# The order of the 24 attention-times-value products inside a unit: h's products by a table of four orders for each place, l's products drawn at random

## The chip, the cores and the metric

The kernel runs on one core of one Trainium2 chip. The metric is the device time of one execution in microseconds, the median of several. The core's engines run their own instruction streams side by side: TensorE (PE, with its weight loads shown apart as PEld), VectorE (DVE), ScalarE (ACT), GpSimd (POOL) and SyncE (SP); the last two issue most of the DMA transfers here.

## What is computed

For each of B = 4 images, with N = 64 x 64 = 4096 positions and C = 256 channels:

```python
q = einsum('bwhc,cd->bwhd', x, Wq) + bq      # d = 128
k = einsum('bwhc,cd->bwhd', x, Wk) + bk
v = einsum('bwhc,cd->bwhd', x, Wv) + bv      # d = 256
pq, pk, pv = q.reshape(B, -1, N), k.reshape(B, -1, N), v.reshape(B, -1, N)
energy = einsum('bcn,bcm->bnm', pq, pk)
attention = softmax(energy, axis=-1)
out = einsum('bcm,bnm->bcn', pv, attention).reshape(B, W, H, C)
return gamma * out + x
```

All of it is in float32. The kernel uses TensorE's faster float32 form (`F32R`) and gets its accuracy back by splitting numbers into parts: the attention weights of a unit are held as three tiles h, l and d, and the values as three arrays `vh`, `vl` and `vd`.

## The kernel before

**Tiling.** An image's 4096 output columns are cut into 16 groups of 256 (`NG`, `NB`; two halves j of 128, `NJ` = 2). For every group the 4096 positions m that are summed over are gone through in 8 units (`NU`) of four blocks of 128 positions each. So an image has 128 units (`STEPS`) and the program 512. A unit's number in its group, t = u mod 8, is called its *place*.

**What a unit does.** TensorE makes 12 products for the energies of the unit three ahead (`energy`, line 330, 256 columns each), and 24 products in `attend` (line 383): eight with weights from h, eight from l, eight from d. ScalarE takes the exponentials of the energies (line 334) and makes h (line 349); VectorE joins the two exponentials (line 344) and makes l (line 355) and d (line 358). GpSimd's queue loads the next k tile (line 314).

**The 24 products.** Each is one load of 128x128 weights and one matmul. The weights are `left[:, i, j*P:(j+1)*P]`: block i of 0 to 3, half j of 0 or 1. What streams through them is one row of the value array, `right[:, m, ...]` with `m = 2*t + i//2 + 16*(i%2)`; both halves j of a block i stream the same row. For h and l the row is 258 columns wide (256 values and two ones, which sum up the softmax's denominator) and goes to `acc[j]`, a PSUM tile for each half; for d it is 256 wide and goes to `bb`. `vh` and `vl` hold rows of `VC` = 260 float32, that is 1040 bytes, so that a row's start, in bytes, is 16 m beyond a multiple of 1024; `vd` holds rows of 256 float32, 1024 bytes, so that all its rows start alike. Blocks i = 0 and 1 of a unit (m = 2t and 2t + 16) start equally far, modulo 256 bytes, and i = 2 and 3 (m = 2t + 1 and 2t + 17) start 16 bytes further; they are called L and H below.

**The order before.** For each of h, l, d: first half j = 0 with i = 0, 1, 2, 3, then j = 1 with i = 0, 1, 2, 3. Written as digits x = 4 j + i this is 01234567, as starts it is LLHHLLHH. One exception is written in the code (`back`): in l's products of places 1 and 3 the second half goes i = 3, 2, 1, 0.

**What sets the order around it.** The whole kernel runs under a manual schedule: each engine's queue holds its instructions in the order in which the program writes them. In the loop over units (lines 509 to 551) it is: energies of u + 3, first half; join and upper of u + 2; energies, second half; load of k; a piece of an earlier group's `finish`; `halves` of u + 1; `attend(u)`; another piece of `finish`. At a group's last unit (t = 7) ScalarE copies `acc[0]` and `acc[1]` out (line 394). The pieces of `finish` then run on the other engines: VectorE reads `bb` (line 404) in the next unit, ScalarE scales (line 407), and TensorE transposes the result (line 415) after `attend` of place 1. `finish_last` (lines 427 to 464) does the same for the very last group.

Of the kernel before, what the change touches and what calls it, by code (L numbers as in the profile page):

```python
# [2 lines left out]

# [17 lines left out]
def kernel(  # L21
# [36 lines left out]
    nc = tc.nc  # L58
    B, W, H, C = x.shape
    P = 128  # L60
# [4 lines left out]
    NI = NM // 2  # L65
# [108 lines left out]
    NJ = NB // P  # L174
    NG = N // NB
    NU = NM // 4
# [22 lines left out]
    with ExitStack() as fast:  # L199
# [18 lines left out]
        vh = qkv.tile([P, NM, VC], F32R, tag="vh", name="vh")  # L218
        vl = qkv.tile([P, NM, VC], F32R, tag="vl", name="vl")
        vd = qkv.tile([P, NM, C], F32R, tag="vd", name="vd")  # L220
# [131 lines left out]
        def halves(b, u):  # L352
# [7 lines left out]
            )  # L360
            units[b, u] = h, l, d

        def attend(b, u):

            g, t = divmod(u, NU)
            if t == 0:
                now["acc"] = [
                    ps_o.tile([P, C + 2], F32, tag=f"a{j}", name=f"a{j}_{b}_{g}")
                    for j in range(NJ)
                ]  # L370
                now["bb"] = ps_o.tile([P, NJ, C], F32, tag="bb", name=f"bb_{b}_{g}")
            h, l, d = units[b, u]
            acc, bb = now["acc"], now["bb"]
            for left, right in ((h, vh), (l, vl), (d, vd)):
                for j in range(NJ):
                    out_ = bb[:, j, :] if left is d else acc[j]


                    back = left is l and j == NJ - 1 and t in (1, 3)
                    for i in reversed(range(4)) if back else range(4):  # L380
                        m = 2 * t + i // 2 + NI * (i % 2)

                        nc.tensor.matmul(  # L383
                            out_,
                            left[:, i, j * P : (j + 1) * P],
                            right[:, m, : out_.shape[1]],
                            start=(t == i == 0 and (left is h or left is d and j == 0)),
                            stop=(t == NU - 1 and i == 3 and left is not h),
                            skip_group_check=True,
                        )  # L390
            if t == NU - 1 and (b, g) != (B - 1, NG - 1):
                o = now["o"] = work.tile([P, NJ, C + 2], F32, tag="o", name=f"o_{b}_{g}")
                for j in range(NJ):
                    nc.scalar.activation(o[:, j, :], acc[j], AF.Identity, scale=1.0 + E)
# [89 lines left out]
        for b in range(B):  # L484
# [24 lines left out]
            for u in range(STEPS):  # L509
                g, t = divmod(u, NU)  # L510
# [33 lines left out]
                for forms in beside:  # L544
                    next(forms)
                attend(b, u)
                if (b, u) == (B - 1, STEPS - 1):
                    finish_last(b, g, loads.pop((b, "x", g)))
# [10 lines left out]
    NG = N // NB  # L559
    NJ = NB // P  # L560
    NP = NM // 2
    xg, og = columns(x, NB), columns(out, NB)
    with tc.If(nc.values_load(again[0:1, 0:1]) > 0), ExitStack() as general:
# [8 lines left out]
        for b in range(B):  # L572
# [16 lines left out]
            for g in range(NG):  # L589
                ps = []  # L590
                mx = work.tile([P, 2, NB], F32, tag="mx", name=f"gmx_{b}_{g}")
                for t in range(NP):
                    sp = ps_s.tile([P, 2, NB], F32, tag="s", name=f"gs_{b}_{g}_{t}")
                    for h in range(2):
# [4 lines left out]
                            start=True,  # L599
                            stop=True,  # L600
# [31 lines left out]
                for t, p in enumerate(ps):  # L632
# [8 lines left out]
                    for h in range(2):  # L641
                        for s in range(2):
# [4 lines left out]
                                start=(t == h == 0),  # L647
                                stop=(2 * t + h == NM - 1),
# [43 lines left out]
```

## Time and profile before

| what | value |
|---|---|
| median of 8 runs | 2449.4 us (2447.75 to 2450.61) |
| the profiled execution's own time | 2449.84 us |
| span of its trace, first to last instruction | 2448.1 us |
| mean granted TensorE clock | 0.998 |
| PE busy | 2436.4 us, 19988 matmuls |
| PEld busy | 2405.0 us |
| DVE busy | 2100.5 us |
| ACT busy | 1795.9 us |
| POOL busy | 424.5 us |

Busy time of TensorE is the union of its matmuls' stretches; the matmuls are pipelined, so each row's duration (282 ns for a 258-column one) is longer than the time by which it moves the next one on. That time is read from the start of one matmul to the start of the next, and is called a *step* below. The trace gives every matmul's start to the nanosecond; a sum of 23 steps is the time from a unit's first product of h to its last product of d.

### The profile page before, as it was taken

The numbers are of one execution on the slowest core, as the hardware profiler recorded it, in microseconds if no ns is written. First come the engines' busy times: TensorE is split into PE (matmuls) and PEld (weight loads), VectorE is DVE, ScalarE is ACT, GpSimd is POOL, SyncE is SP. The second block draws the span as 40 slices with busy tenths as digits, with TensorE's granted clock in tenths as the row PEclk, the third lists the DMA queues.
The fourth block names the chain that finished last, engine by engine and source line by source line (L and its number), as shares of the span: only waits on it lengthen the run. The fifth ranks groups of instructions, "written<-read, shape, count | busy, mean of one in ns | idle before, by whom it ended". The sixth has DMA issues, their size and how long they took to land.

```text
span 2448.1 us, 50042 instructions
## 1 busy us (share of the span) xinstructions
PE 2436.4 (100%) x19988; PEld 2405.0 (98%) x19988; DVE 2100.5 (86%) x2318; ACT 1795.9 (73%) x3201; POOL 424.5 (17%) x781
## 2 busy tenths in 40 slices
PE   9999999999999999999999999999999999999998
PEld 8999999999899999999989999999998999999998
DVE  5988888888698888888869888888886988888887
ACT  5877777777677777777667777777766777777775
POOL 4211111111411111111141111111114111111110
PEclk9999999999999999999999999999999999999999
DMA  7666666665776666666476666666647766666663
GB/s 230 215 210 204 210 206 198 210 207 160 227 224 202 205 212 204 205 203 208 151 241 222 202 202 212 203 207 200 209 142 246 230 204 198 210 204 211 206 202 113
DMA packets 137407, 498.92 MB, mean 204 GB/s; under 512 B 15536, under 2 KB 57264, under 8 KB 137168
## 3 DMA queue, kind: packets, MB, share of 16 engines
q0 software_dynamic: 92320, 453.17, 58.8%
q1 hardware_dynamic: 44304, 42.22, 5.5%
q8 instruction: 160, 2.62, 0.4%
q14 instruction: 79, 0.65, 0.1%
q10 hardware_dynamic: 544, 0.26, 0.0%
HBM read 445.25 MB, written 50.33 MB: 202 GB/s over the span
## 4 chain that ended last, share of the span: by engine, by line
PE 99%; DMA 0%; DVE 0%; SPq 0%; issue 0%
PE a L383 40%; PE bb L383 19%; PE sa L330 19%; PE sb L330 10%; PE qk L135 5%; PE v L156 5%; PE xt L122 1%; PE ot L415 1%; DMA x<-in_x_dram 0%; SPq L82 0%; DVE o L452 0%; PE ot L457 0%; DVE x L463 0%; PE zp L449 0%; DVE r L441 0%
## 5 line engine op out<-in xcount | busy, mean ns | idle before, releaser
L334 ACT ACTIVATE x<-sa 128x512 f32<-128x512 f32 x1024 | 612.3, 598 | 510.0 <-PE sa L330 507.8
L344 DVE TENSOR_TENSOR x<-x,y 128x1024 f32<-128x1024 f32 x512 | 626.7, 1224 | 228.5 <-ACT y L334 228.4
L330 PE MATMUL sa<-q,k 128*128 128x256 f32 x4096 | 733.2, 279 | 0.0
L358 DVE SCALAR_TENSOR_TENSOR d<-h,x 128x1024 fp32r<-128x1024 f32 x512 | 623.9, 1219 | 0.0
L355 DVE TENSOR_TENSOR l<-x,h 128x1024 fp32r<-128x1024 f32 x512 | 623.8, 1218 | 0.0
L330 PEld LDWEIGHTS sa<-q,k 128*128 128x128 f32 x4096 | 617.9, 188 | 0.6 <-ACT x L334 0.2
L334 ACT ACTIVATE y<-sb 128x512 f32<-128x512 f32 x1024 | 616.4, 602 | 0.0
L383 PE MATMUL a<-vh,h 128*128 128x258 f32 x4096 | 574.3, 282 | 0.0
L383 PE MATMUL a<-vl,l 128*128 128x258 f32 x4096 | 571.9, 282 | 0.0
L330 PE MATMUL sb<-q,k 128*128 128x256 f32 x2048 | 566.2, 276 | 0.0
L383 PE MATMUL bb<-vd,d 128*128 128x256 f32 x4096 | 556.3, 278 | 0.0
L314 POOL DMA_DIRECT2D k<-kf x512 | 278.9, 545 | 1568.0 <-PE sb L330 1539.4
L349 ACT ACTIVATE h<-x 128x1024 fp32r<-128x1024 f32 x512 | 544.2, 1063 | 8.6 <-DVE x L344 8.1
L383 PEld LDWEIGHTS a<-vl,l 128*128 128x128 f32 x4096 | 524.6, 189 | 0.0
L383 PEld LDWEIGHTS a<-vh,h 128*128 128x128 f32 x4096 | 522.7, 189 | 0.0
L383 PEld LDWEIGHTS bb<-vd,d 128*128 128x128 f32 x4096 | 513.7, 188 | 0.0
L330 PEld LDWEIGHTS sb<-q,k 128*128 128x128 f32 x2048 | 384.9, 188 | 0.1
L135 PE MATMUL qk<-wqk_sb,xts 128*128 128x256 f32 x512 | 122.7, 383 | 0.0
L156 PE MATMUL v<-xts,wv_sb 128*128 128x256 f32 x512 | 120.3, 379 | 0.0
L156 PEld LDWEIGHTS v<-xts,wv_sb 128*128 128x128 f32 x512 | 97.3, 190 | 13.2
L135 PEld LDWEIGHTS qk<-wqk_sb,xts 128*128 128x128 f32 x512 | 93.2, 192 | 10.4
L275 POOL DMA_DIRECT2D qd<-qks x128 | 69.2, 549 | 180.9 <-DVE qks L144 171.9
(60 smaller groups left out, 868.7 us busy)
## 6 DMA issues: line engine op xcount, KB each, us to landing
k<-kf POOLq DMA_DIRECT2D x512, 768.0 KB, 4.6
x<-in_x_dram SPq DMA_DIRECT2D x128, 256.0 KB, 3.8
kf<-f POOLq DMA_DIRECT2D x64, 384.0 KB, 3.8
out_dram<-x POOLq DMA_DIRECT2D x63, 256.0 KB, 2.5
qd<-qks POOLq DMA_DIRECT2D x128, 64.0 KB, 2.7
qr<-qd SPq DMA_DIRECT2D x64, 128.0 KB, 3.5
wv_sb<-in_L_conv_Wv_dram POOLq DMA_DIRECT2D x1, 256.0 KB, 7.2
out_dram<-x SPq DMA_DIRECT2D x1, 256.0 KB, 3.6
```

The costliest lines, as they stand in the source:

```text
L122: nc.tensor.transpose(tp[:, k, s, :], self.xs[i][:, s, k * P : (k + 1) * P], ident,)
L135: nc.tensor.matmul(qk[:, s, :], self.xt[i][:, k, s, :], wqk_sb[:, k, :], start=(k == 0), stop=(k == KC - 1),)
L156: nc.tensor.matmul(vp[:, eh, :], wv_sb[:, k, eh * P : (eh + 1) * P], self.xt[i][:, k].rearrange("p s a -> p (s a)"), start=(k == 0), stop= ...
L275: nc.gpsimd.dma_start(qd[b, i // 2 + NG // 2 * s][:, i % 2, :], x[:, s, :C2])
L314: nc.gpsimd.dma_start(t.rearrange("p (i s) f d -> p i s (f d)", s=2), kf[b, u % NU])
L330: nc.tensor.matmul(to[:, i], kt[:, 2 * k + i, f, :], q[:, f], start=first, stop=last)
L334: nc.scalar.activation(to[:, 2 * k : 2 * k + 2, :], sp.rearrange("p i j d -> p i (j d)"), AF.Exp, scale=scale,)
L344: nc.vector.tensor_tensor(x, x, y, ALU.mult)
L349: nc.scalar.activation(h, units[b, u], AF.Identity, scale=UPPER)
L355: nc.vector.tensor_tensor(l, x, h.bitcast(F32), ALU.subtract)
L358: nc.vector.scalar_tensor_tensor(d, h.bitcast(F32), 1.0 + E, x, ALU.mult, ALU.subtract)
L383: nc.tensor.matmul(out_, left[:, i, j * P : (j + 1) * P], right[:, m, : out_.shape[1]], start=(t == i == 0 and (left is h or left is d and ...
```

## The change

Each of h, l and d now goes through all eight products (j, i) in an order of its own: d in 01234567 as before; h in one of four orders written out for each place, the group's number deciding which (so each of the four is used in 16 of a place's 64 units); l in an order drawn with a fixed seed. l's draw takes, for each unit, one of the 70 ways of giving four of the eight positions to L (x in 0, 1, 4, 5) and four to H (x in 2, 3, 6, 7), no way twice in a place, and shuffles within L and within H. So the two halves j, and with them the two PSUM tiles, are mixed. The exception for places 1 and 3 goes. The `start` mark stands on the first product that goes to each PSUM bank in a group, as before; the `stop` mark on the last two of l and of d in the group's last unit, where it stood on the last of each half. The number of instructions, their shapes and their data are the same.

```diff
-from itertools import cycle
+from itertools import combinations, cycle
+from random import Random
...
+        UPPERS = (
+            ('13564072', '20356471', '40257316', '53461702'),
+            ('41256307', '75401632', '20537164', '04537216'),
+            ('26147053', '14360725', '47051623', '53710624'),
+            ('41236075', '45207631', '51204673', '65032471'),
+            ('10436572', '10642357', '47036521', '10275634'),
+            ('57164203', '06341752', '53410627', '53704162'),
+            ('35042176', '34076512', '64507213', '65437201'),
+            ('35210467', '43605172', '20751364', '62137054'),
+        )
+        chance = Random(11)
+        halves_of_8 = list(combinations(range(8), 4))
+        lowers = [chance.sample(halves_of_8, B * NG) for _ in range(NU)]
+
+        def order(f, b, g, t):
+            if f == 2:
+                return "01234567"
+            if f == 0:
+                return UPPERS[t][(b * NG + g) % len(UPPERS[t])]
+            low, high = chance.sample("0145", 4), chance.sample("2367", 4)
+            first = lowers[t][b * NG + g]
+            return [(low if x in first else high).pop() for x in range(8)]
+
         def attend(b, u):
...
-            for left, right in ((h, vh), (l, vl), (d, vd)):
-                for j in range(NJ):
+            begun = set()
+            for f, (left, right) in enumerate(((h, vh), (l, vl), (d, vd))):
+                for n, x in enumerate(order(f, b, g, t)):
+                    j, i = divmod(int(x), 4)
                     out_ = bb[:, j, :] if left is d else acc[j]
-                    back = left is l and j == NJ - 1 and t in (1, 3)
-                    for i in reversed(range(4)) if back else range(4):
-                        m = 2 * t + i // 2 + NI * (i % 2)
-                        nc.tensor.matmul(
-                            out_,
-                            left[:, i, j * P : (j + 1) * P],
-                            right[:, m, : out_.shape[1]],
-                            start=(t == i == 0 and (left is h or left is d and j == 0)),
-                            stop=(t == NU - 1 and i == 3 and left is not h),
-                            skip_group_check=True,
-                        )
+                    bank = 2 if left is d else j
+                    m = 2 * t + i // 2 + NI * (i % 2)
+                    nc.tensor.matmul(
+                        out_,
+                        left[:, i, j * P : (j + 1) * P],
+                        right[:, m, : out_.shape[1]],
+                        start=(t == 0 and bank not in begun),
+                        stop=(t == NU - 1 and n >= 6 and left is not h),
+                        skip_group_check=True,
+                    )
+                    begun.add(bank)
```

## The prediction

> **What bounds the kernel.** I read the page's first two parts and its chain, then the waits of TensorE, then the groups of line 383, then the timeline of TensorE over one unit.
>
> ```profile
> span 2448.1 us, 50042 instructions
> PE 2436.4 (100%) x19988; PEld 2405.0 (98%) x19988; DVE 2100.5 (86%) x2318; ACT 1795.9 (73%) x3201; POOL 424.5 (17%) x781
> PEclk9999999999999999999999999999999999999999
> PE 99%; DMA 0%; DVE 0%; SPq 0%; issue 0%
> ```
>
> TensorE is busy in all of the span, the clock is full throughout, and the chain that ended last is 99% TensorE.
>
> ```profile
> PE xt L122 <- DMA x<-in_x_dram: 2.1, 1, 2.1
> PE wp L197 <- DVE ones L88: 1.1, 1, 1.1
> PE zp L449 <- DVE zs L447: 0.5, 1, 0.5
> PE ot L457 <- DVE o L452: 0.2, 1, 0.2
> ```
>
> This is the whole list of what TensorE waited for: 3.9 us, all at the two ends. No unit waits for h, l, d, k or a PSUM tile. So the time is a sum of steps (start to start), and only a change of steps can change it.
>
> ```profile
> L383 PE MATMUL a<-vh,h x4096: 276/283/366, 77.3 to 2436.3; 128*128 128x258 f32 x196
> L383 PE MATMUL a<-vl,l x4096: 276/282/288, 78.2 to 2437.2; 128*128 128x258 f32 x196
> L383 PE MATMUL bb<-vd,d x4096: 276/276/287, 79.2 to 2438.1; 128*128 128x256 f32 x196
> ```
>
> Minimum, median and maximum duration, ns. The 258-column products vary between 276 and 288, the 256-column ones sit at the floor.
>
> ```profile
> 302.37 0.28 PE L330 MATMUL sb<-q,k 128*128 128x256 f32 x1
> 302.49 1.12 PE L383 MATMUL a<-vh,h 128*128 128x258 f32 x8
> 303.44 1.11 PE L383 MATMUL a<-vl,l 128*128 128x258 f32 x8
> 304.39 0.87 PE L383 MATMUL bb<-vd,d 128*128 128x256 f32 x6
> ```
>
> Start, length, products: h's block moves the queue on by 0.95 us, l's by 0.95.
>
> **Steps, from the single starts in the trace.** Summed over the program: h 491.0 us (119.9 ns each of 4096), l 488.6 (119.3), energies 113.3 each in most units. Median of one place's 64 units, ns:
>
> place 0 to 7, h's eight steps: 957, 958, 955, 951, 954, 957.5, 973, 963 (mean 958.6)
> l's eight steps: 956, 952, 953, 957, 956, 952.5, 944, 963 (mean 954.2)
> all 23 steps of the unit: 2721, 2727, 2713, 2714, 2727, 2727, 2720, 2733 (mean 2722.8)
>
> At one place one position repeats within 1 ns in most units, whichever of h's three buffers is used and whatever VectorE and ScalarE do; between positions and places it runs from 113 to 125 ns. So a step hangs on the rows' starts and on the order, and the order is a lever on 32 us: (491.0 + 488.6) us less 8192 x 115.7 ns (d's mean step, 473.9 us / 4096).
>
> **The change, part by part.** It removes and adds no instruction, byte or wait; it moves matmuls inside a block of eight.
>
> *h's eight products.* Neither the orders nor mixed halves are in this trace, so I bound them by rows. Cut into blocks of four, the 32 blocks (h and l, two halves, eight places) have medians from 468 to 488 ns, mean 478, and the lowest six average 470.5. If all h blocks were the dearest, 2 x 488 = 976 would be +17.4 a unit; the cheapest, 936, would be -22.6. At which end the table's orders lie no row can say: that they are called measured is no evidence, so it is a case and not a finding. In the forecast they lie at the low end, two blocks of 470, hence 940: -18.6 ns; in rivals 2 and 4 they don't. Not all of it stays. At place 6 h is 14.4 above the mean and l and d are below by as much and more, so that the unit's sum is 2720, under the mean. Over the eight places a least-squares line gives 0.26 ns of unit for 1 ns of h's block; all kept would be 1. I take the middle, 0.63: -11.7 ns a unit, ends -18.6 and 0.
>
> *l's eight products.* A random order has no choice in it. Class by class, the mean steps of the present order are L to L 119.2, H to H 121.0, L to H 119.6, H to L 118.4. A step between two different starts (119.0) is thus 1.1 cheaper than between equal ones (120.1); a random order has 3.43 equal neighbours of 8 where the present one has 4, so -0.6 ns a unit. On the other side the turned-round halves of places 1 and 3 go: their sums, 2727 and 2714, stand beside 2727 and 2733 for places 5 and 7, whose rows start alike modulo 64 bytes; at most 0 and 19 ns are lost, 2.4 a unit over eight places, and I take half, +1.2. Ends: 2 x 488 = 976 against 954.2, +21.8; and 936, -18.
>
> *Mixed halves and PSUM tiles.* Energies alternate a, a, b between two PSUM tiles at 113.3 a step, with no step dearer at the change of tile; d stays within one at the same 113. Cost 0; bound: 16 steps of 2 ns if it did cost, 16 us, which the rows speak against.
>
> *Release of acc.* The copies of line 394 now may wait for l's last product for both halves. Their row: the first copy begins 472 ns after l's last start, so already behind it; the second ends 1239 ns before the next group's first product of h. Cover 1.2 us, cost 0; without cover 63 groups would each pay the excess. At the very end, acc[0] can be ready four steps later, 0.48 us at most, while d's eight products still run: 0.
>
> *After the transposes.* At place 2 the energies follow line 415's transposes and fall into one of two rhythms: 113.3 ns a step, or 117.8 (in 28 of 64 units), 56 ns a unit dearer. What place 1 leaves behind may tip it: all 64 would be +2.0 us, none -1.6. I take 0.
>
> *The engines behind.* A unit of some 4190 ns has DVE busy for 1224 + 1218 + 1219 = 3661 and ACT for 2 x 598 + 2 x 602 + 1063 = 3463: 10 ns less leaves both their cover. SP's and POOL's queues keep their order.
>
> Sum: -11.7 - 0.6 + 1.2 = -11.1 ns a unit, times 512 is -5.7 us. The profiled execution took 2449.84 us (span 2448.1 and 1.7 around it), 0.4 above the median: 2444.1 beside it, 2443.7 beside the median. I say 2444.
>
> **A rule that speaks against it.** A 258-column step is 119.6 ns in the mean here and moves with the order of starts. The Trainium skill, "TensorE: Matmul & The Clock Gate", section "Back-to-back issue gap", gives a warm step as the columns over 2.4 GHz plus 2.5 ns and names no order and no start address: about 110.0 ns for 258 columns by that formula, an estimate from the page. By it the order could not matter and the sum would be 0, 2449.4 us; the trace shows steps of 114 and 125 for one shape.
>
> **Rivals.**
>
> 1. *Given back within the unit.* h's gain goes as at place 6, and l pays what it lost. For: 0.26 rather than 1. Then -18.6 x 0.26 = -4.8, plus 1.2, less 0.6: -4.2 ns, -2.2 us: 2447.2. Against: blocks end in d's even rhythm, and unit sums do differ by 20 ns.
>
> 2. *The random l is dear (slower).* The present order keeps two equal starts together. If lone starts between others, hardly seen here, cost what place 7 shows in each unit, the sum is 2733 against 2722.8 everywhere: +10.2 ns, +5.2 us, 2454.6 when h gives nothing. It decides as soon as l's mean block lies over 954.2 by more than h keeps: over 966 at 11.7 kept. For: both of place 7's blocks are at 963. Against: the class means differ by 2.6 ns only.
>
> 3. *More than that.* All of h's 18.6 kept and l at its present 954: -9.5 us, 2439.9. For: totals of 2713 occur with h at 955, so h at 940 may leave units near 2700. Against: the whole lever would have to be found in one half of the products.
>
> 4. *The table does nothing* (its orders are ordinary ones): -0.6 + 1.2 = +0.6 ns, +0.3 us: 2449.7.
>
> **How the numbers follow.** Forecast (h kept by half or more, 2441 to 2447) 0.50; rival 1 with 4, 0.20; rival 2, 0.20; rival 3, 0.10. The limit of what a measurement tells from no change is 0.2%, 4.9 us: 2444.5. A little over six tenths of the forecast lies below it, 0.32, and rival 3's 0.10: faster 0.42. The rest of the forecast and rivals 1 and 4: 0.38. Rival 2 counts as slower: 0.20, some of it at or below 2454.3. The range goes from rival 3, with 1.6 us for the rhythm after the transposes, to half of rival 2: 2438 to 2453. The forecast's own range is 2441 to 2447.
>
> **What would show it.** Right: h's mean block near 940 and l's near 954, the 23 steps' mean near 2712, nothing new among TensorE's waits, d's steps from the third on still 113. Wrong: h's mean block at 955 or more; a wait on `o` (line 394) at place 0; l's mean above 966; or h short and the unit's sum unchanged.

## The result: slower by 0.3%, and where the time went

The changed kernel takes 2456.66 us (median of 11 runs, 2456.2 to 2458.31) against 2449.58 us (31 runs): a ratio of 1.0031, 95% interval 1.0023 to 1.0039. The forecast was 2444.0, with a range of 2438 to 2453. The profiled execution of the changed kernel took 2454.96 us, less than any of the eleven, so that the differences read from the two traces below are some 2 us smaller than that of the medians.

The first lines of its page, its share of engines on the chain that ended last, and then all that TensorE waited for:

```profile
span 2453.2 us, 50041 instructions
PE 2441.6 (100%) x19988; PEld 2410.8 (98%) x19988; DVE 2100.3 (86%) x2318; ACT 1797.1 (73%) x3201; POOL 425.8 (17%) x781
PEclk9999999999999999999999999999999999999999
PE 98%; DMA 1%; ACT 0%; issue 0%; DVE 0%; POOL 0%; SPq 0%; POOLq 0%; DVEq 0%; ACTq 0%
```

```profile
PE xt L123 <- DMA x<-in_x_dram: 1.8, 1, 1.8
PE wp L198 <- DVE ones L89: 1.1, 1, 1.1
PE zp L475 <- DVE zs L473: 0.9, 1, 0.9
PE ot L483 <- DVE o L478: 0.2, 1, 0.2
```

Nothing new is waited for (4.0 us at the two ends, as before); TensorE's busy time has grown by 5.2 us, the span by 5.1. So the steps have grown. The products of line 408, which was line 383 (minimum, median and maximum duration, ns):

```profile
L408 PE MATMUL a<-vh,h x4096: 276/281/370, 75.7 to 2441.2; 128*128 128x258 f32 x196
L408 PE MATMUL a<-vl,l x4096: 276/282/301, 76.6 to 2442.2; 128*128 128x258 f32 x196
L408 PE MATMUL bb<-vd,d x4096: 275/279/297, 77.6 to 2443.1; 128*128 128x256 f32 x196
```

h's median fell by 2 ns. d's rose from 276 to 279, though d's order, rows and shapes are what they were. The steps from start to start, summed over the program and compared between the two profiled executions, show the whole of it:

| steps of | before, us | after, us | difference |
|---|---|---|---|
| h | 491.0 | 487.2 | -3.8 |
| l | 488.6 | 489.9 | +1.3 |
| d | 473.9 | 476.8 | +2.9 |
| energies, sa | 474.8 | 479.3 | +4.5 |
| energies, sb | 233.0 | 235.1 | +2.1 |
| q and k projections (line 136) | 112.2 | 110.6 | -1.6 |

9.5 us were added in products that the change does not touch. The last row is no effect of the change: the profiled execution before had a short stretch of lower granted clock near its start (0.93 and 0.90 in the first two stretches of 10 us, steps of 427 ns in the first q and k products), the other had none (1.00 and 1.00, steps of 216 ns). Without that row the differences add up to 7.0 us, and the medians differ by 7.1.

Here is TensorE's timeline over place 7 of one group of the changed kernel: start, length, then the products.

```profile
172.00 0.39 PE L331 MATMUL sa<-q,k 128*128 128x256 f32 x2
172.23 0.28 PE L331 MATMUL sb<-q,k 128*128 128x256 f32 x1
172.34 0.39 PE L331 MATMUL sa<-q,k 128*128 128x256 f32 x2
...
173.37 1.11 PE L408 MATMUL a<-vh,h 128*128 128x258 f32 x8
174.31 1.13 PE L408 MATMUL a<-vl,l 128*128 128x258 f32 x8
175.28 1.11 PE L408 MATMUL bb<-vd,d 128*128 128x256 f32 x8
176.23 0.40 PE L331 MATMUL sa<-q,k 128*128 128x256 f32 x2
176.47 0.28 PE L331 MATMUL sb<-q,k 128*128 128x256 f32 x1
176.58 0.40 PE L331 MATMUL sa<-q,k 128*128 128x256 f32 x2
...
177.64 1.12 PE L408 MATMUL a<-vh,h 128*128 128x258 f32 x8
```

The products at 173.37 are place 7's. Before h's block the twelve energies take 173.37 - 172.00 = 1.37 us; after d's block the next twelve take 177.64 - 176.23 = 1.41. They are the same instructions on the same kind of tiles. In between lie h and l, whose order left TensorE in another rhythm: 117.8 ns a step instead of 113.3. The granted clock is 1.00 from 172.00 to 177.64 us; it is not the clock. The eleven steps between a unit's twelve energies sum to 1247 ns in the one rhythm and 1296 in the other, with almost nothing between (64 units are longer by their first step, which follows transposes or projections). A unit whose energies go in the second rhythm is called slow below, in the first fast. Of the 500 units that have twelve energies right before their products, 33 are slow in the kernel before, and 147 in the changed one. By the rhythm in which a unit leaves TensorE's queue, which is that of the next unit's energies, a unit of places 0 and 2 to 7 takes 4190.7 ns from its first product to the next unit's when it leaves it fast (4194.6 before), and 4261.3 when it leaves it slow: 70.6 ns dearer. 128 such units make 9.0 us.

### The profile page after: what moved, and what is told of

It is laid out like the page before. It is cut to its first block, busy times and chain, and to the rows that moved or that the text cites. A ratio compares the mean times of both kernels' runs of the same rounds, so it can differ in the third digit from the quotient of the medians.

```text
span 2453.2 us, 50041 instructions
## 1 busy us (share of the span) xinstructions
PE 2441.6 (100%) x19988; PEld 2410.8 (98%) x19988; DVE 2100.3 (86%) x2318; ACT 1797.1 (73%) x3201; POOL 425.8 (17%) x781
## 4 chain that ended last, share of the span: by engine, by line
PE 98%; DMA 1%; ACT 0%; issue 0%; DVE 0%; POOL 0%; SPq 0%; POOLq 0%; DVEq 0%; ACTq 0%
PE a L408 40%; PE bb L408 19%; PE sa L331 19%; PE sb L331 10%; PE qk L136 4%; PE v L157 4%; PE ot L441 1%; PE xt L123 1%; DMA kf<-f 0%; DMA x<-in_x_dram 0%; ACT v L166 0%; ACT vh L293 0%; DVE qks L145 0%; ACT f L264 0%; DVE vd L297 0%
```

## The experiments

All ratios are against the kernel before, run on the same chip; the intervals are 95%.

**h's table alone.** l keeps the order before.

```diff
-            low, high = chance.sample("0145", 4), chance.sample("2367", 4)
-            first = lowers[t][b * NG + g]
-            return [(low if x in first else high).pop() for x in range(8)]
+            return "01237654" if t in (1, 3) else "01234567"
```

> h in the changed kernel's table, l in the order before (with the turned-round halves of places 1 and 3). Theory (l's random order leaves TensorE's queue in the slow rhythm, 282.7 cycles a step instead of 272, through d and the next unit's energies, 70 ns a unit): h's block stays near 951.6 ns (-7.3 a unit, -3.7 us), energies are slow in some 30 to 60 units as before, time 2443 to 2448. Rival A (the h table, with its mixed halves and PSUM tiles, is what tips the rhythm): energies slow in 100 units or more, time about 2455. Rival B (the two are additive and l's steps are dear by themselves): 2446 with h and l blocks as in the two kernels.

2451.59 us, ratio 1.0010 (1.0001 to 1.0019). h's block is 950.7 ns, as expected, but 108 units are slow, as many as rival A gave, at a time that it did not give. The theory, that the random l tips the rhythm and h's table doesn't, fell: h's table does it too. Sorted by place and by which of the four orders h has, slow is close to all or none: after place 6, 16 of 16 units with 35042176 and 16 of 16 with 34076512, and none with the other two; after place 3, 16 of 16 with 51204673 and none with the rest; after place 0, none with any. Only three of the 32 groups are mixed.

**l's random orders alone.** h goes in 01234567.

> h in 01234567, l in the changed kernel's random orders. Theory: h's block 958.9 ns as before, l's near 957, energies slow in 120 to 180 units, time 2456 to 2462 (the changed kernel's 2456.7 plus h's 3.7 us). Rival A: energies slow in at most 50 units, time near 2451.

2459.94 us, ratio 1.0043 (1.0029 to 1.0056). h 958.8 ns, l 956.8, 147 slow units. As expected by the theory, but after the run above both parts tip the rhythm, and the new theory is: the whole sequence of h and l, on the rows of that place, fixes a unit's time and the rhythm in which it leaves the queue.

**The best pairs seen, one for each place.** Edit of `order` (f is 0 for h, 1 for l; the lines that it replaces are left out here):

```diff
+            return (
+                ("53461702", "17045632"), ("41256307", "41327065"),
+                ("26147053", "06527134"), ("65032471", "57041623"),
+                ("47036521", "75364201"), ("53410627", "43075126"),
+                ("35042176", "16247305"), ("35210467", "50176243"),
+            )[t][f]
```

> One pair of orders (h's, l's) for each place, the same in all groups: of the changed kernel's units that came out of the fast rhythm and left the queue in it, the shortest of each place. Theory (a unit's time is fixed by the place, the two orders and the rhythm it starts in, and by nothing else): the units take 4180, 4166, 4146, 4160, 4180, 4160, 4174 ns at places 0 and 2 to 7 and the 23 steps 2700 at place 1, 28 ns a unit less than before, 14 us: 2433 to 2439. Rival C (which unit runs fast is chance, or hangs on the data or on other engines): the pairs give units like the changed kernel's mean, 2450 to 2457.

2436.49 us, ratio 0.9949 (0.9936 to 0.9963): faster than both kernels, within the forecast 2433 to 2439. The 23 steps average 2696.1 ns (2722.9 before) and 32 units are slow. All 32 come after transposes or projections. Outside them nearly every unit of a place agrees with the others within 1 ns in its 23 steps, at a pair of orders that ran once in the changed kernel, so chance, data and other engines are out.

**Slow pairs.** The same edit with pairs of units that had started and ended slow.

> One pair for each place, of the units that started in the slow rhythm and left the queue in it, the longest of each place. Theory: once in the slow rhythm the units stay there; energies slow in most of the 500 units, 70 to 90 ns a unit more: 2480 to 2495. If the rhythm is seldom entered: as many slow units as the transposes of place 1 start, time 2455 to 2475. Rival C: 2450 to 2460.

2463.32 us, ratio 1.0056 (1.0038 to 1.0075); 192 slow units, fewer than the 2480 to 2495 needed; the time lies in the range given for a rhythm that is seldom entered. Again all or none: all the units of places 0, 4 and 5 start slow, and of the others none but four of place 2. Pairs that had ended slow from a slow start leave the queue fast from a fast one. So the rhythm in which a unit starts belongs to what fixes its end. It is not all of it: at places 0 and 5 the pairs start slow here as they did in the changed kernel, where they left slow, and all of them leave fast. Fast and slow do not describe a start in full; what else belongs to it no run shows.

**The starts of l kept, its blocks and halves at random.** h in 01234567, and

```diff
-            first = lowers[t][b * NG + g]
+            first = (0, 1, 4, 5)
```

> h in 01234567; l's starts in the order LLHHLLHH in all units, but which of the two blocks and halves of the same start comes first is drawn at random. Theory with starts alone (a unit's time hangs on the sequence of row starts; blocks, halves and PSUM tiles do not count): every unit of a place alike, at places 0, 2, 4, 5, 6 and 7 like before (23 steps 2721, 2713, 2727, 2727, 2720, 2733), slow energies only in about 30 units, time 2448 to 2452. Rival D (which weights or which PSUM tile come next counts too): the units of a place differ by 7 ns and more and slow energies come and go within a place, time 2452 to 2460.

2454.86 us, ratio 1.0020 (1.0010 to 1.0031), above what the theory gave and inside what rival D gave, yet its units are not D's. At places 0 and 5 every one of the 16 steps of h and l agrees with the kernel before within 1 ns in every unit, though each unit mixes blocks, halves and PSUM tiles in another way. Here the sequence of starts alone counts. The 5 us come from the two places where the kernel before had its turned-round halves: at place 3 the 23 steps are 2742 ns in place of 2713, and all 64 units leave the queue slow, 53 ns more before place 4; at place 1, 12 ns. 64 x (28 + 53 + 12) = 6.0 us; 1.2 come back at place 2, where 4 units are slow and not 28.

**The best starts, other blocks.** The best pairs with the digits of each start made ascending: ("02134657", "02145367") for place 0, and so on.

> The pairs of the run with the best pairs, kept in their sequence of starts alone: which of the two blocks and halves with the same start comes first is made ascending. Theory with starts alone: units as there (h 948, l 949, 23 steps 2696), 2435 to 2438. Rival D: blocks and halves count after all, and units fall back towards 2722, 2440 to 2457.

2436.36 us, ratio 0.9945 (0.9931 to 0.9958); 99.8% of h's and l's steps within 2 ns of the run with the best pairs. The blocks that changed places start 16 x 1040 bytes apart, which is 65 x 256: starts that agree modulo 256 bytes are alike. Its page:

```profile
span 2432.6 us, 50042 instructions
PE 2421.4 (100%) x19988; PEld 2390.6 (98%) x19988; DVE 2099.7 (86%) x2318; ACT 1796.2 (74%) x3201; POOL 424.5 (17%) x781
```

The same 19988 matmuls, 15.0 us less of TensorE's busy time than before.

**What about the starts makes a step long?** Four runs with one suspicion each. Rows of 1088 bytes, so that all start alike modulo 64 bytes (`VC = C + 16`; to make room, one f tile instead of two), with the changed orders, with those before, and the control with one f tile and rows of 1040:

> The changed kernel with rows of vh and vl 1088 bytes apart instead of 1040, so that all rows start alike modulo 64 bytes (and one f tile instead of two, to make room, which touches the projections alone). Theory (the steps' spread and the tipping come from rows that start 16, 32 or 48 bytes off): h's and l's steps become equal whatever the order, within 2 ns, the slow rhythm is as rare as after the transposes of place 1 (about 30 units), and this kernel's units equal those of the next run's. Rival E (the spread comes from the 258 columns, which do not fill a multiple of 16, or from the order of weights): spread and slow units stay, 120 or more.

> The kernel before with the same rows of 1088 bytes and one f tile. Theory: h and l blocks equal at all eight places, and equal to those of the run above; time within 3 us of it. Rival E: blocks differ between places, and the two runs differ by about 7 us as the two kernels do.

> The kernel before with one f tile and rows of 1040 bytes: a control for the two runs above. Units as before; the projections of 64 pieces may wait for the f tile, 0 to 15 us in all.

2522.62, 2531.3 and 2506.28 us (ratios 1.0298, 1.0337, 1.0234). The one f tile costs 57 us around the projections, not 15 at most, and hides nothing of the units: the control's blocks are those of the kernel before. With rows of 1088 bytes h's blocks are dearer in the mean, not cheaper, steps still run from 114 to 125 ns, slow units number some 148 and 280, and with the order before they still come place by place. Alignment modulo 64 bytes does not make steps equal, and the theory that it would fell. But the differences between places went almost wholly: with the order before h's block is now 962 or 963 ns at all eight places (951 to 973 with 1040 bytes), and the 23 steps are 2746 ns at every even place, 2723 at 5 and 7, and 2737 at 1 and 3 with their turned-round halves.

> The changed kernel with 256 columns instead of 258 in all of l's products and in h's at places 1 to 7 (leaves out most of the sum of the softmax's denominators); rows stay 1040 bytes apart, so starts stay uneven. Rival F (two columns over 256 cost a further fetch and let the queue slip): h's and l's steps fall to 113 to 116 whatever the order, no slow rhythm but after place 1, 2410 to 2422. Theory with uneven starts: steps still differ between orders by several ns and slow energies still come by order in 60 units or more, time above 2425.

```diff
-                        out_,
+                        out_ if left is d or (t == 0 and left is h) else out_[:, :C],
...
-                        right[:, m, : out_.shape[1]],
+                        right[:, m, : C + 2 if t == 0 and left is h else C],
```

2448.62 us, ratio 0.9995 (0.9985 to 1.0005). Against the changed kernel two columns less take 5 ns (h) and 12 ns (l) off a block, but its steps run from 113 to 126 ns and 164 units are slow. It is not the two columns.

> The changed kernel with rows of 1088 bytes, all rows starting alike modulo 64 bytes, and 272 columns in h's and l's products, a whole multiple of 16 (the 14 further columns are ones that nobody reads), one f tile. Rival F: h's and l's steps all equal, about 120 ns, slow energies only after place 1's transposes; time as the control with one f tile plus at most 5 us, 2500 to 2512. Otherwise spread and slow units stay as with 258 columns, 2518 to 2535.

2566.05 us, ratio 1.0473, above both ranges: the 14 further columns lengthen h's and l's steps by 83 ns a unit against the run with 258 columns, 43 us. Steps run from 120 to 134 ns and 137 units are slow. Not the multiple of 16 either.

**Rows of 1024 bytes, all one start.** `VC = C`, and for the denominators

```diff
+        row = qkv.tile([P, C + 4], F32R, tag="row", name="row")
...
-                        out_,
+                        out_ if left is d or (t == i == 0 and left is h) else out_[:, :C],
...
-                        right[:, m, : out_.shape[1]],
+                        row[:, : C + 2] if t == i == 0 and left is h else right[:, m, :C],
```

> The changed kernel's orders with rows of vh and vl 1024 bytes apart, as vd's are, and 256 columns; the softmax's denominators come from a row of ones that takes the place of the values of block 0 at place 0 (so the values of that block and the other blocks' share of the denominators are left out). Theory G (a step depends on the starts' distance modulo 1024 bytes, not modulo 64, and rows one pitch of 1024 apart all count as one start): h's and l's steps fall to d's 113.3 ns whatever the order, blocks of 907, 23 steps near 2607, slow energies only after place 1's transposes, time 2383 to 2395. Rival H (the order of the weights, h's and l's tiles, makes the spread): spread of 113 to 125 and 100 slow units or more remain, time above 2430.

2456.96 us, ratio 1.0030 (1.0020 to 1.0040). Half of theory G holds: the order has lost its effect, at places 3 to 5 h's and l's blocks are 939 and 937 ns with a spread of 0.5 to 1.0 over units that all have different orders. The other half fell: steps are 117 ns, not 113.3, in h, l and d alike. The energies just before them are back at 113.3 (six in 229.32 - 228.64 = 0.68 us, then blocks of 0.94):

```profile
228.64 0.39 PE L332 MATMUL sa<-q,k 128*128 128x256 f32 x2
228.87 0.28 PE L332 MATMUL sb<-q,k 128*128 128x256 f32 x1
228.98 0.39 PE L332 MATMUL sa<-q,k 128*128 128x256 f32 x2
229.21 0.28 PE L332 MATMUL sb<-q,k 128*128 128x256 f32 x1
229.32 1.10 PE L409 MATMUL a<-vh,h 128*128 128x256 f32 x8
230.26 1.10 PE L409 MATMUL a<-vl,l 128*128 128x256 f32 x8
231.20 1.10 PE L409 MATMUL bb<-vd,d 128*128 128x256 f32 x8
```

What else had moved was the weights. The row of ones and the narrower rows put all that is allocated behind them 32 bytes further.

> As the run with rows of 1024 bytes, with a padding tile 16 bytes smaller, so that all that lies behind it (the weights' tiles x, y, h, l, d, k and q among them) starts where it does in the kernel before; there it had moved by 16 bytes. Leaves out the same values and denominators. Theory (the slow rhythm of that run came from weights that start 16 bytes off): steps of 113.3 ns in h, l and d whatever the order, 23 steps near 2607, time 2385 to 2400. Rival (one start for all rows settles the order's effect but not the rhythm): steps stay at 117, time 2445 to 2460.

2457.27 us, and 98.6% of the units' 23 steps as in the run before within 1 ns: this padding moved nothing, which fits addresses given out in steps of 32 bytes. It says nothing on the question but that the run repeats.

> The kernel before with a padding tile 16 bytes larger: the weights' tiles and q start 16 bytes further, no order changed. Theory: the rhythm is a matter of where weights and rows start, so energies leave 113.3 ns and the time moves by over 5 us, probably up, 2455 to 2480. Rival (where the weights start does not count): 2447 to 2452.

Here the step of 32 bytes was made, in the kernel before, without any change of order (`[P, 20]` for `[P, 16]` in the first padding tile): 2480.05 us, ratio 1.0125 (1.0108 to 1.0142), 284 slow units, the 23 steps at 2748.3 ns. Where the tiles behind the padding start counts too. Among them are the weights h, l, d and k, but also q, which streams through the energies, so this run alone does not say which of them it is.

> As the run with rows of 1024 bytes, with a padding tile 32 bytes smaller (addresses are given out in steps of 32 bytes, so the 16 bytes of the run before moved nothing): the weights' tiles h, l, d, k and q now start where they do in the kernel before. Leaves out the same values and denominators. Theory (two things set the rhythm, the starts of the rows and those of the weights; the slow one in that run came from weights 32 bytes further): steps of 113.3 ns in h, l and d whatever the order, 23 steps near 2607, slow energies only after place 1's transposes, time 2385 to 2400. Rival (the rhythm does not hang on the weights' start): steps stay at 117, 2445 to 2460.

2415.50 us, ratio 0.9862 (0.9846 to 0.9879). The time is not that of a whole kernel, since values and denominators are left out; with 256 columns and rows of 1040 bytes it was 2448.62. The kernel differs from the run with rows of 1024 bytes in the padding alone: there h's, l's and d's steps averaged 117.3 ns at places 3 to 7 right after energies that were back at 113.3, though k and q had moved too. So of what TensorE reads in these products it is the start of h, l and d that counts. With one start for all rows and these weights where they were, the units have two speeds and almost nothing between. Place 7 of one group and place 5 of the next on TensorE's timeline:

```profile
173.41 0.39 PE L332 MATMUL sa<-q,k 128*128 128x256 f32 x2
173.64 0.28 PE L332 MATMUL sb<-q,k 128*128 128x256 f32 x1
...
174.77 1.07 PE L409 MATMUL a<-vh,h 128*128 128x256 f32 x8
175.68 0.96 PE L409 MATMUL a<-vl,l 128*128 128x256 f32 x7
```

```profile
198.87 0.40 PE L332 MATMUL sa<-q,k 128*128 128x256 f32 x2
199.10 0.28 PE L332 MATMUL sb<-q,k 128*128 128x256 f32 x1
...
200.28 1.11 PE L409 MATMUL a<-vh,h 128*128 128x256 f32 x8
201.22 0.99 PE L409 MATMUL a<-vl,l 128*128 128x256 f32 x7
```

Energies 1.36 us and h's block 0.91, against 1.41 and 0.94. In 46 of the 64 groups h's and l's steps at places 3 to 6 average 113.4 ns, in 18 they average 117.8. The rhythm changes at the transposes after place 1 and then lasts to the group's end, whatever orders h and l have. All 18 slow groups hand it on to the next group: 14 of these keep it until their own transposes, four lose it at place 0, where two of h's products stream the row of ones. That is why it took 2415 us and not the 2385 to 2400 expected: some 146 units with 36 steps at 4.5 ns more are about 24 us. With equal starts, at places 2 to 7, no order leads into the slow rhythm, and none leads out of it.

## Why the prediction was wrong

**What bounds the kernel: right.** The time is a sum of steps; apart from 4 us at the ends nothing is waited for before or after. The clock was not quite "full throughout" in the trace before: the 0.93 and 0.90 at its start are 1.7 us lost, which the page's 40 slices do not show.

**h's eight products: right way, smaller.** -11.7 ns a unit predicted, the block fell by 7.3 (958.9 to 951.6 in the mean), not to 940. Two of the lowest blocks of four seen before do not make a block of eight.

**l's eight products: too small.** +0.6 predicted, +2.5 measured. The class means of the order before (119.0 between different starts, 120.1 between equal ones) said little on other sequences.

**The turned-round halves: the bound was wrong.** The prediction gave at most 19 ns at place 3, from the 23 steps of place 7, whose rows start alike modulo 64 bytes. The run with l's starts kept shows 28 ns in the 23 steps and 53 in the energies that follow, and 12 at place 1, where the bound was 0. Both errors are in it: modulo 64 bytes was the wrong likeness, and the sum stopped at d.

**The step that failed: "After the transposes ... I take 0".** The slow rhythm was seen, and its price a unit was right (56 ns predicted in the energies; 70.6 with d's part). But its cause was placed in the transposes alone, so it was bounded by place 2's 64 units, -1.6 to +2.0 us. The runs show that sequences of starts can leave TensorE in it at every place: 147 slow units, and 9.5 us in d and the energies. Of the 12.7 us between forecast and result these are 9.5; h's and l's steps make the other 3.2. The sum of 23 steps, which the prediction took for a unit, moved from 2722.9 to 2722.2 ns: inside that window d gave back most of what h had won, and the net loss lies behind it. The trace before held a sign of it: d's rows all start alike and its order never changes, yet its first four steps run from 113 to 124 ns by place before they settle, so what was streamed before reaches into later products. The prediction read d as an even 113. Rival 2 had the sign and nearly the size (2454.6), but looked for them inside the 23 steps; its test, an l block over 966 ns, did not come true. In the 23 steps it was nearest to rival 1, given back.

**Mixed halves, the release of acc, the engines behind: 0, right.** With the sequence of starts kept, mixing blocks, halves and PSUM tiles changes no step by more than 1 ns at places 0 and 5, and 99.8% of all steps of the best starts by at most 2; no wait on `acc` or `o` appeared at place 0.

**The rule weighed.** A step of columns over 2.4 GHz plus 2.5 ns (the Trainium skill, "TensorE: Matmul & The Clock Gate", section "Back-to-back issue gap") would have given no change. The section offers it as the gap of an isolated matmul and says that in a stream of loads and matmuls both set the step, so it was not made for this stream. The runs speak against it as an account of this stream: the same 19988 matmuls took 2436.4, 2456.7 and 2463.3 us in three orders.

What stays open: why a start makes a step longer, what in TensorE the two rhythms are, and what besides the rhythm a unit hands on to the next. That uneven row starts modulo 64 bytes, the two odd columns and the multiple of 16 do not by themselves make the spread and the slow units is shown; that starts of rows and of weights both count is shown; the mechanism between them is not.

## What to carry to other kernels

When one engine is busy in all of the span, measure its work from start to start and follow the sum past the edited block until the steps are back in their old rhythm: a change of order can be paid for by untouched instructions behind it. An order that is fast in one place is not fast in another; where steps repeat to the nanosecond, pick whole sequences from a trace (here h and l together, with the rhythm in which they start and end; the fast pairs held, the slow ones did not), and expect them to hold only as long as no tile moves. Give streamed rows one common start where the layout allows it: then the order is free, though not yet fast (2457.0 us here with the weights 32 bytes further, 2415.5 with them back).

## What was not expected of the hardware

- A stream of equal weight loads and matmuls of 256 columns has two lasting rhythms, 113.3 and 117.8 ns a step at the full granted clock, and stays in the one it is in from a group's transposes to its end when all rows start alike (46 groups fast, 18 slow).
- The order of eight products moves a 258-column step between 113 and 126 ns by the sequence of row starts; with that kept, blocks, halves and PSUM tiles don't count, and a sequence repeats within 2 ns.
- A shift of the weights, and of all else behind one padding tile, by 32 bytes, with no order changed, cost 30.6 us of 2449.5 us (ratio 1.0125); with rows of 1024 bytes it was 41.5 us (2457.0 against 2415.5).
